# The softmax shift of an attention layer as a 33rd contraction row, with queries and keys stored and loaded as such rows

## The chip, the cores and the metric

The kernel runs on one core of a Trainium2 chip. Its time is the device time of one execution in microseconds, the median of several runs. All arithmetic of four layers is in this one launch; the inputs and the output lie in device memory (HBM).

The core's engines work side by side, each through its own queue in order: PE (TensorE: matrix products, with PEld for its weight loads), DVE (VectorE), ACT (ScalarE), POOL (GpSimd) and SP (SyncE, which here issues nearly all DMAs).

## The reference, cut to what matters

An image of 32 x 32 positions (L = 1024) with C = 256 channels, four images (NB = 4), passes four layers: a convolution with a state-space scan, a grouped convolution, an attention over the 1024 positions with a mixture of experts behind it, and a second scan with a second mixture of experts. The change touches the attention of layer 2 only:

```python
Q, K, V = (proj(Wq, bq), proj(Wk, bk), proj(Wv, bv))      # 8 heads of 32
scores = jnp.einsum('bhnd,bhmd->bhnm', Q, K) / jnp.sqrt(jnp.float32(hd))
mask = jnp.zeros((N, N), dtype=bool).at[edge_index[0], edge_index[1]].set(True)
scores = jnp.where(mask[None, None], scores, -jnp.inf)
attn = jax.nn.softmax(scores, axis=-1)
attended = jnp.einsum('bhnm,bhmd->bhnd', attn, V)
```

The softmax subtracts a number from each query's scores before the exponential. Any number gives the same result as long as nothing overflows. The kernel uses zero, unless a bound on the scores says that they could be large; then it takes the row's maximum.

## The kernel before

**The scans.** Both scans are cut into units of 128 rows x 1024 positions, 1280 in all. A unit takes DVE a product with PE's replicated rows (`ps_rep`) and a running scan (`h<-dA,ps_rep`), ACT an exponential (`dA`), POOL a product, PE two products for `ps_rep` and, every second unit, eight records of collecting products (`ps_y`). Its `dA` is a DMA of 512 KB, loaded four units ahead into one of five buffers. The order of the scans is fixed (`SCANS`, line 32; a pair is layer and image): (0,0), (0,1), (3,0), (0,2), (3,1), (0,3), (3,2), (3,3). A scan of layer 0 has 256 units, one of layer 3 has 64. So (3,3) begins at unit 1216.

**The side stages.** All else is written as Python generators and laid between the units (`STAGES`, line 34): `front` of an image before its first scan; `middle` between its two scans (the end of layer 0, layer 1, attention, experts, and the beginning of layer 3, `front3`); `last` after its second scan (the end of layer 3 and its experts). One stage runs at a time and isn't broken off; when it ends, `advance` (line 598) picks the first stage in the list whose scan is done, or, failing that, one whose scan is far enough. `middle` of image 3 must deliver the inputs of scan (3,3). When they aren't there at unit 1216, `need` (line 583) lays the whole rest of that stage down without scans between; in that stretch, `alone` is set and attention uses the scans' PSUM (`ps_sx` instead of `ps_sc`).

**The clocks kept by hand.** How densely side work is laid between units is decided when the program is written, not on the chip. `Metered` (line 99) adds an estimated cost to a clock per engine for each instruction. `run` (line 620) goes through the scans' half units and calls `advance` at most twice in each, only while no engine's clock is ahead of the vector clock. A tensor product's estimate is `matmul_us`:

```python
us = 0.46e-3 * columns(out)
if lhsT.dtype != BF16:
    us = max(4 * us, 0.3)
if out.shape[0] <= 32:
    return us / 4
return us / 2 if lhsT.shape[0] <= 32 else us
```

**Attention** (`attention`, line 1264). Queries and keys are projected into `qT` and `kT` (128 partitions x 2 x 1024: four heads of 32 rows in each half), the bound on the scores is worked out (`large_scores`), the mask is loaded as additive bf16 tiles (`maskT`), values are projected. POOL then adds two biases. `shift` (line 1406) holds a branch: with small scores nothing is done and `mT`, the shift, stays at zero; with large ones `row_max` fills it, each number split into three bf16 parts in rows of their own. In the traced execution no instruction of `row_max` ran.

`all_heads` (line 1328) then runs 64 steps: two halves of the queries (`nh`), four pairs of heads (`hp`), eight blocks of 128 keys (`kb`). A step of `heads` (line 1478) has on PE: two products of 32 rows for the scores of the pair, two products of 32 rows of ones (`onesb`) with the shift, two of 128 rows that add the mask; ACT takes the exponential into `p`; two steps later four products of `p` with values and with ones, 32 columns each, are summed over the blocks (`ps_at`). SP has nothing to do in these steps but the scans' DMAs.

Of the kernel before, what the change touches and what calls it, by code (L numbers as in the profile page):

```python
# [8 lines left out]
F32 = mybir.dt.float32  # L9
BF16 = mybir.dt.bfloat16  # L10
I32 = mybir.dt.int32
AF = mybir.ActivationFunctionType
ALU = mybir.AluOpType
# [4 lines left out]
P = 128  # L18
NB = 4
L = 1024  # L20
TB = L // P
C = 256
DI = 512
DC = DI // P
HEADS, HD = 8, 32
# [117 lines left out]
class Hybrid:  # L143
# [1092 lines left out]
    def prepare2(self, st):  # L1236

        nc, vec = self.nc, self.vec
        self.gamma, self.beta, self.bo = (self.rows("L2_attn_" + n) for n in ("gamma", "beta", "bo"))
        wo = self.weight(st, "L2_attn_Wo", 2)  # L1240
        yield
        ps = self.ps("ps_bo", (P, C))
        for k in range(2):
            nc.tensor.matmul(
                ps, lhsT=vec["L2_attn_bv"][:, k : k + 1].to_broadcast([P, P]), rhs=wo[:, k, :],
                start=(k == 0), stop=(k == 1),
            )
        nc.vector.tensor_tensor(self.bo, self.bo, ps, ALU.add)
        self.isq = 1.0 / float(HD) ** 0.5
        self.bq = self.const.tile([P, 2], F32, name="bq_")  # L1250
        nc.vector.tensor_scalar(self.bq, vec["L2_attn_bq"], self.isq, None, ALU.mult)

        byhead = st.tile([P, 4], F32, name="byhead4")
        nc.vector.tensor_reduce(
            byhead, self.ident.rearrange("p (h d) -> p h d", d=HD), AX.X, ALU.add
        )
        self.byhead = self.const.tile([P, 4, 8], F32, name="byhead")
        nc.vector.tensor_copy(self.byhead, byhead.unsqueeze(2).to_broadcast([P, 4, 8]))
        self.onesb = self.const.tile([P, P], BF16, name="onesb")
        nc.vector.memset(self.onesb, 1.0)  # L1260
        self.ones = self.const.tile([P, 32], F32, name="ones32")
        nc.vector.memset(self.ones, 1.0)

    def attention(self, b, tb):
        nc, tc, vec = self.nc, self.tc, self.vec
        with tc.tile_pool(name=f"at{b}", bufs=1, side="right") as op:
            xa = op.tile([P, TB, C], F32, name="xa")
            qT = op.tile([P, 2, L], F32, name="qT")
            kT = op.tile([P, 2, L], F32, name="kT")
            v = op.tile([P, TB, C], F32, name="v")  # L1270
            mT = op.tile([P, 2, L], BF16, name="mT")
            maskT = op.tile([P, TB, L], BF16, name="maskT")
            wo = self.weight(op, "L2_attn_Wo", 2)
            large = op.tile([1, 1], I32, name="large")
            nc.vector.memset(mT, 0.0)
            with tc.tile_pool(name=f"aa{b}", bufs=1, side="right") as fp:
                wq, wk, wv = (self.weight(fp, "L2_attn_" + n, 2) for n in ("Wq", "Wk", "Wv"))
                xT = fp.tile([P, 2, L], F32, name="xTa")
                yield from self.norm(fp, tb, TB, xa, "lnt")
                yield from self.turned(xa, TB, xT)  # L1280

                def project(item):
                    w, dst, bias, sc, c, g = item
                    ps = self.ps("ps_qk")
                    cols = slice(g * 512, (g + 1) * 512)
                    self.mm(ps, lambda k: w[:, k, c * P : (c + 1) * P], xT, 2, cols)
                    nc.scalar.activation(
                        dst[:, c, cols], ps, AF.Identity, bias=bias[:, c : c + 1], scale=sc
                    )

                yield from self.pipe(
                    [
                        (w, dst, bias, sc, c, g)
                        for w, dst, bias, sc in (
                            (wq, qT, self.bq, self.isq), (wk, kT, vec["L2_attn_bk"], 1.0)
                        )
                        for c in range(2) for g in range(2)
                    ],
                    project, cost=1.7,
                )  # L1300

                yield from self.large_scores(fp, qT, kT, large)
                for _ in self.mask_work:
                    pass
                nc.sync.dma_start(maskT, self.mem[("maskT",)].rearrange("j p f -> p j f"))

                def values(j):
                    ps = self.ps("ps_v", (P, 2, C))
                    for i in range(2):
                        m = 2 * j + i  # L1310
                        for k in range(2):
                            nc.tensor.matmul(
                                ps[:, i, :], lhsT=xT[:, k, m * P : (m + 1) * P], rhs=wv[:, k, :],
                                start=(k == 0), stop=(k == 1),
                            )
                    nc.scalar.copy(v[:, 2 * j : 2 * j + 2, :], ps)

                yield from self.pipe(range(TB // 2), values, cost=1.7)
            go = nc.values_load(large, engines=self.sides, min_val=0, max_val=1)
            tc.mark_branch_hint_location(f"large{b}", go, engines=self.sides)  # L1320
            yield from self.add_rows(xa, self.bo, TB)
            yield from self.add_rows(tb, self.beta, TB)
            with tc.tile_pool(name=f"ab{b}", bufs=1, side="right") as fp:
                yield from self.shift(fp, qT, kT, mT, maskT, go, f"large{b}")
            with tc.tile_pool(name=f"ac{b}", bufs=1, side="right") as fp:
                yield from self.all_heads(b, fp, tb, qT, kT, v, maskT, mT, xa, wo)

    def all_heads(self, b, fp, tb, qT, kT, v, maskT, mT, xa, wo):
        nc = self.nc

        def divided(raw, sums, c):
# [8 lines left out]
        halves = [  # L1340
            [fp.tile([P, 2, 512], F32, tag=t, name=t, bufs=2) for t in ("raw", "sums")]
            for _ in range(2)
        ]
        scores, values = self.heads(fp, halves, qT, kT, v, maskT, mT)
        for n in range(len(steps) + 2):
            if n >= 2:
                values(steps[n - 2])
# [10 lines left out]
            nh, hp, kb = steps[n - 2]  # L1358
# [58 lines left out]
    def row_max(self, fp, qT, kT, mT, mask):  # L1417


        nc = self.nc  # L1420

        m3 = fp.tile([P, TB, HEADS, 32], BF16, name="m3")
        nc.vector.memset(m3, 0.0)
        mx = fp.tile([P, TB, HEADS, 2], F32, name="mx")
        got = {}
        yield 1.0
# [19 lines left out]
        def largest(item):  # L1446
# [8 lines left out]
            scores, largest, cost=1.4,  # L1455
        )
        m = fp.tile([P, TB, HEADS], F32, name="mneg")
        nc.vector.tensor_reduce(m, mx, AX.X, ALU.max, negate=True)
        for s in range(3):
            nc.vector.tensor_copy(m3[:, :, :, s], m)  # L1460
            if s < 2:
                nc.vector.tensor_tensor(m, m, m3[:, :, :, s], ALU.subtract)
        yield 1.0

        def turn(item):
            c, g = item
            ps = self.ps("ps_m3", dtype=BF16)
            for k in range(4):
                nc.tensor.transpose(
                    ps[:, k * P : (k + 1) * P],  # L1470
                    m3[:, 4 * g + k, 4 * c : 4 * c + 4, :].rearrange("p h s -> p (h s)"),
                    self.identb,
                )
            nc.scalar.copy(mT[:, c, g * 512 : (g + 1) * 512], ps)

        yield from self.pipe([(c, g) for c in range(2) for g in range(2)], turn, cost=0.8)

    def heads(self, fp, halves, qT, kT, v, maskT, mT):

        nc = self.nc
        got, acc = {}, {}

        def scores(step):
            nh, hp, kb = step
            qs = slice(nh * 512, (nh + 1) * 512)
            c, at = hp // 2, 64 * (hp % 2)
            alone = self.alone  # L1490
            if alone:
                both = self.scan_psum.tile([P, 2, 512], F32, tag="x", name="ps_sx", bufs=2)
                two = [both[:, i, :] for i in range(2)]
            else:
                two = [self.psum.tile([P, 512], F32, tag="s", name="ps_sc", bufs=2) for _ in range(2)]
            rows = [slice(at + 32 * i, at + 32 * i + 32) for i in range(2)]
            for i in range(2):
                nc.tensor.matmul(
                    two[i], lhsT=kT[rows[i], c, kb * P : (kb + 1) * P], rhs=qT[rows[i], c, qs],
                    start=True, stop=False,  # L1500
                )
            for i in range(2):
                nc.tensor.matmul(
                    two[i], lhsT=self.onesb[rows[i], :], rhs=mT[rows[i], c, qs],
                    start=False, stop=False,
                )
            got[step] = p = fp.tile([P, 2, 512], F32, tag="p", name="p", bufs=3)
            for i in range(2):
# [659 lines left out]
```

## Time and profile before

| | us |
|---|---|
| median of 3 runs | 6310.74 |
| lowest, highest | 6305.61, 6317.68 |
| profiled execution | 6294.21 |
| span of its instructions | 6292.5 |
| PE, DVE, ACT, POOL busy | 5142.7, 5032.7, 3410.6, 3825.9 |
| 512 records of the shift's products, busy (404 `ps_sc`, 108 `ps_sx`) | 86.1 + 20.6 |
| first and last scores of image 0, 1, 2 | 1400.6 to 1644.2, 2461.9 to 2702.9, 3826.4 to 4071.2 |
| first and last scores of image 3 | 5192.6 to 5388.2 |
| last unit before (3,3), first and last of (3,3) | 5227.8, 5680.7 and 5954.8 |

An f32 product stands in the trace as two records. Busy time of an engine counts overlapping records once. Units can be counted in the trace as scans on DVE (`h<-dA,ps_rep`), and a stage's place in units by the scans that began before its first instruction. Every side instruction carries the line of the helper that meters it (L131), so groups are told apart by the names of their tiles.

### The profile page before, as it was taken

Reading aid. Unit: us, or ns where it says so; the run is one execution under the profiler, and the core shown is the slowest. Engines: PE = TensorE matmul, PEld = TensorE weight load, DVE = VectorE, ACT = ScalarE, POOL = GpSimd, SP = SyncE. Lnnn points to the kernel's source line nnn. Section 1 sums busy time; section 2 is a strip of 40 time slices with the busy share of each in tenths; the row PEclk is TensorE's granted clock in tenths of the full one; section 3 lists DMA queues with packets and bytes.
Section 4 is the critical chain, followed back from the end, with each engine's and each line's share of the span. In section 5 each row is a group of like instructions: output and inputs, shape, how many; then the busy total and the mean of one; then the engine's idle time right before and its main releaser. Section 6 shows DMA issues by size and latency. Waiting matters only on the chain. (4 is left out here: it accounts for less than half of the span.)

```text
span 6292.5 us, 59823 instructions
## 1 busy us (share of the span) xinstructions
PE 5142.7 (82%) x20249; PEld 2117.1 (34%) x20249; DVE 5032.7 (80%) x4016; ACT 3410.6 (54%) x4299; POOL 3825.9 (61%) x1948
## 2 busy tenths in 40 slices
PE   5676785579798568979869969989689779997999
PEld 2122120132253122234225522244145332543566
DVE  5888898988898998889889988899889982317811
ACT  3565655345496435558638735567547544336621
POOL 2787768665586766568767756577867752006600
PEclk7687785589798668979969979979779889999989
DMA  3555555544355656445455576345545761027611
GB/s 109 160 158 167 165 175 185 159 150 136 113 173 177 194 165 170 132 128 191 159 178 174 182 179 165 119 150 195 174 156 179 208 161 48 19 73 184 166 34 34
DMA packets 347915, 934.97 MB, mean 149 GB/s; under 512 B 37748, under 2 KB 120256, under 8 KB 345984
## 3 DMA queue, kind: packets, MB, share of 16 engines
q1 hardware_dynamic: 344880, 928.38, 48.7%
q0 software_dynamic: 2128, 2.13, 0.2%
q8 instruction: 165, 2.70, 0.2%
q14 instruction: 166, 1.36, 0.1%
q10 hardware_dynamic: 576, 0.39, 0.0%
HBM read 841.02 MB, written 92.37 MB: 148 GB/s over the span
## 5 line engine op out<-in xcount | busy, mean ns | idle before, releaser
L131 POOL TENSOR_TENSOR h<-h,rows 128x1024 f32<-128x1024 f32 x1280 | 3024.2, 2366 | 1740.4 <-DVE h L131 1529.3
L131 DVE TENSOR_TENSOR_SCAN h<-dA,ps_rep 128x1024 f32<-128x1024 f32 x1280 | 2924.3, 2285 | 182.2 <-ACT dA L131 53.6
L131 DVE TENSOR_TENSOR ps_rep<-ps_rep,rows 128x1024 f32<-128x1024 f32 x1280 | 1549.4, 1210 | 142.6 <-PE ps_rep L131 141.7
L131 PE MATMUL ps_rep<-S,spread_L_conv_A_log 96*128 96x512 bf16 x2048 | 752.8, 456 | 770.3 <-DVE h L131 722.4
L131 ACT ACTIVATE dA<-dA,A_L_conv_A_log 128x1024 f32<-128x1024 f32 x1024 | 1125.4, 1142 | 440.0 <-DMA dA<-dt 405.7
L131 PE MATMUL ps_y<-h,collect_L_conv_A_log 128*32 128x512 f32 x4096 | 704.4, 741 | 15.3 <-POOL h L131 15.3
L131 PE MATMUL ps_e<-we,h_m 128*128 128x256 f32 x3072 | 709.4, 383 | 8.3 <-ACT h_m L131 8.3
L131 PEld LDWEIGHTS <-spread_L_conv_A_log 96*128 96x128 bf16 x2048 | 159.7, 102 | 1558.0 <-DVE h L131 1246.4
L131 PEld LDWEIGHTS ps_e<-we,h_m 128*128 128x128 f32 x3072 | 583.3, 191 | 159.2 <-ACT h_m L131 31.0
L131 PE MATMUL ps_h<-xTm,we 128*128 128x512 f32 x1280 | 603.3, 607 | 4.6 <-DMA we<-in_L_ffn_W_dram 4.5
L131 ACT ACT_TABLE_LOAD x402 | 515.8, 1283 | 37.0 <-PE ps_h L131 15.5
L131 ACT ACTIVATE h_m<-ps_h,cols 128x512 f32<-128x512 f32 x384 | 257.5, 686 | 423.0 <-PE ps_h L131 421.0
L131 ACT ACTIVATE p<-ps_sc 128x512 f32<-128x512 f32 x404 | 219.3, 594 | 316.7 <-PE ps_sc L131 306.1
L131 ACT ACTIVATE dA<-dA,A_L_attn_A_log 128x1024 f32<-128x1024 f32 x256 | 282.8, 1143 | 141.4 <-DMA dA<-dt 122.8
L131 PEld LDWEIGHTS ps_h<-xTm,we 128*128 128x128 f32 x1280 | 242.2, 193 | 281.0 <-issue 211.5
L131 PE MATMUL ps_rep<-S,spread_L_attn_A_log 96*128 96x512 bf16 x512 | 176.8, 433 | 160.2 <-DVE h L131 138.6
L131 PE MATMUL ps_at<-p,v 128*32 128x512 f32 x1024 | 270.7, 608 | 0.2 <-ACT p L131 0.2
L131 PE MATMUL ps_at<-p,ones 128*32 128x512 f32 x1024 | 270.7, 608 | 0.0
L131 DVE SCALAR_TENSOR_TENSOR tb_rows<-ps_e,cw,tb_rows 128x256 f32<-128x256 f32 x128 | 55.7, 477 | 242.8 <-PE ps_e L131 242.7
L131 PE MATMUL ps_sc<-qT,kT 32*128 32x512 f32 x808 | 244.0, 654 | 4.6 <-ACT p L131 2.0
L131 PE MATMUL ps_cv<-pad,diag 128*128 128x512 f32 x504 | 230.5, 597 | 0.0
L131 PEld LDWEIGHTS ps_y<-h,collect_L_conv_A_log 128*32 128x32 f32 x4096 | 93.2, 118 | 339.7 <-issue 216.6
(347 smaller groups left out, 5475.6 us busy)
## 6 DMA issues: line engine op xcount, KB each, us to landing
dA<-dt SPq DMA_DIRECT2D x1280, 512.0 KB
we<-in_L_ffn_W_dram SPq DMA_DIRECT2D x64, 512.0 KB
parts<-parts SPq DMA_DIRECT2D x60, 384.0 KB
S<-parts SPq DMA_DIRECT2D x90, 256.0 KB
dt<-sp_r SPq DMA_DIRECT2D x64, 256.0 KB
y<-yo SPq DMA_DIRECT2D x128, 128.0 KB
y_back<-y SPq DMA_DIRECT2D x64, 256.0 KB
we<-in_L_ffn_w_dram SPq DMA_DIRECT2D x64, 256.0 KB
```

What stands on the lines that cost most here:

```text
L131: return got(*args, **kw)
```

## The change

Queries and keys go to device memory after they are projected, head by head, in blocks of 33 rows: 32 of the head and one more. For keys that row is one (written once, when the kernel starts); for queries it is the shift, written after `shift`. The scores' product then contracts over 33 rows, and its last row adds the shift. The product of ones with the shift is gone, and so are `onesb`, the bf16 parts of the shift in `row_max`, and the long life of `qT` and `kT`, which now stand in a pool of their own that closes before the heads begin. In `heads`, the rows of two heads are loaded into one tile each for keys and queries, at partitions 0 and 64, when a pair's first block begins: for the next pair, and at the very first step for two pairs.

```diff
-        self.onesb = self.const.tile([P, P], BF16, name="onesb")
-        nc.vector.memset(self.onesb, 1.0)
+        one = st.tile([HEADS, L], F32, name="one_row")
+        nc.vector.memset(one, 1.0)
+        self.k_rows = [self.keep(("k", b), [HEADS, HD + 1, L]) for b in range(NB)]
+        for to in self.k_rows:
+            nc.sync.dma_start(to[:, HD, :], one)
...
+                mT = qp.tile([HEADS, L], F32, name="mT")
+                nc.vector.memset(mT, 0.0)
...
+                    for x, to in ((qT, self.q_rows(b)), (kT, self.k_rows[b])):
+                        for h in range(HEADS):
+                            at = HD * (h % 4)
+                            nc.sync.dma_start(to[h, :HD, :], x[at : at + HD, h // 4, :])
+                    yield from self.large_scores(fp, qT, kT, large)
...
+                with tc.tile_pool(name=f"ab{b}", bufs=1, side="right") as fp:
+                    yield from self.shift(fp, qT, kT, mT, maskT, go, f"large{b}")
+                nc.sync.dma_start(self.q_rows(b)[:, HD, :], mT)
...
+        def load(nh, hp):
+            k = fp.tile([P, L], F32, tag="k_rows", name="k_rows", bufs=2)
+            q = fp.tile([P, 512], F32, tag="q_rows", name="q_rows", bufs=2)
+            for i in range(2):
+                at = slice(64 * i, 64 * i + HD + 1)
+                nc.sync.dma_start(k[at, :], self.k_rows[b][2 * hp + i])
+                nc.sync.dma_start(q[at, :], self.q_rows(b)[2 * hp + i, :, nh * 512 : (nh + 1) * 512])
+            rows[nh, hp] = k, q
...
-            rows = [slice(at + 32 * i, at + 32 * i + 32) for i in range(2)]
+            if kb == 0:
+                at = 4 * nh + hp
+                for g in range(0 if at == 0 else at + 1, min(at + 2, 8)):
+                    load(g // 4, g % 4)
+            k, q = rows[nh, hp]
             for i in range(2):
+                of = slice(64 * i, 64 * i + HD + 1)
                 nc.tensor.matmul(
-                    two[i], lhsT=kT[rows[i], c, kb * P : (kb + 1) * P], rhs=qT[rows[i], c, qs],
-                    start=True, stop=False,
-                )
-            for i in range(2):
-                nc.tensor.matmul(
-                    two[i], lhsT=self.onesb[rows[i], :], rhs=mT[rows[i], c, qs],
-                    start=False, stop=False,
+                    two[i], lhsT=k[of, kb * P : (kb + 1) * P], rhs=q[of, :], start=True, stop=False
                 )
```

More of the change, by code (lines that the diff above doesn't have):

```diff
@@ L1267, in attention @@
             xa = op.tile([P, TB, C], F32, name="xa")
-            qT = op.tile([P, 2, L], F32, name="qT")
-            kT = op.tile([P, 2, L], F32, name="kT")
             v = op.tile([P, TB, C], F32, name="v")
-            mT = op.tile([P, 2, L], BF16, name="mT")
             maskT = op.tile([P, TB, L], BF16, name="maskT")
@@ L1274, in attention @@
             large = op.tile([1, 1], I32, name="large")
[L1275 to L1288, printed above, removed]
-                    )
[L1291 to L1295, printed above, removed]
-                        )
[L1297 to L1308, printed above, removed]
-                    for i in range(2):
-                        m = 2 * j + i
-                        for k in range(2):
-                            nc.tensor.matmul(
[L1313 to L1324, printed above, removed]
+            with tc.tile_pool(name=f"aq{b}", bufs=1, side="right") as qp:
+                qT = qp.tile([P, 2, L], F32, name="qT")
+                kT = qp.tile([P, 2, L], F32, name="kT")
+                mT = qp.tile([HEADS, L], F32, name="mT")
+                nc.vector.memset(mT, 0.0)
+                with tc.tile_pool(name=f"aa{b}", bufs=1, side="right") as fp:
+                    wq, wk, wv = (self.weight(fp, "L2_attn_" + n, 2) for n in ("Wq", "Wk", "Wv"))
+                    xT = fp.tile([P, 2, L], F32, name="xTa")
+                    yield from self.norm(fp, tb, TB, xa, "lnt")
+                    yield from self.turned(xa, TB, xT)
+                    def project(item):
+                        w, dst, bias, sc, c, g = item
+                        ps = self.ps("ps_qk")
+                        cols = slice(g * 512, (g + 1) * 512)
+                        self.mm(ps, lambda k: w[:, k, c * P : (c + 1) * P], xT, 2, cols)
+                        nc.scalar.activation(
+                            dst[:, c, cols], ps, AF.Identity, bias=bias[:, c : c + 1], scale=sc
+                        )
+                    yield from self.pipe(
+                        [
+                            (w, dst, bias, sc, c, g)
+                            for w, dst, bias, sc in (
+                                (wq, qT, self.bq, self.isq), (wk, kT, vec["L2_attn_bk"], 1.0)
+                            )
+                            for c in range(2) for g in range(2)
+                        ],
+                        project, cost=1.7,
+                    )
+                    for x, to in ((qT, self.q_rows(b)), (kT, self.k_rows[b])):
[3 more added lines that the diff above has]
+                    yield from self.large_scores(fp, qT, kT, large)
+                    for _ in self.mask_work:
+                        pass
+                    nc.sync.dma_start(maskT, self.mem[("maskT",)].rearrange("j p f -> p j f"))
+                    def values(j):
+                        ps = self.ps("ps_v", (P, 2, C))
+                        for i in range(2):
+                            m = 2 * j + i
+                            for k in range(2):
+                                nc.tensor.matmul(
+                                    ps[:, i, :], lhsT=xT[:, k, m * P : (m + 1) * P], rhs=wv[:, k, :],
+                                    start=(k == 0), stop=(k == 1),
+                                )
+                        nc.scalar.copy(v[:, 2 * j : 2 * j + 2, :], ps)
+                    yield from self.pipe(range(TB // 2), values, cost=1.7)
+                go = nc.values_load(large, engines=self.sides, min_val=0, max_val=1)
+                tc.mark_branch_hint_location(f"large{b}", go, engines=self.sides)
+                yield from self.add_rows(xa, self.bo, TB)
+                yield from self.add_rows(tb, self.beta, TB)
+                with tc.tile_pool(name=f"ab{b}", bufs=1, side="right") as fp:
+                    yield from self.shift(fp, qT, kT, mT, maskT, go, f"large{b}")
+                nc.sync.dma_start(self.q_rows(b)[:, HD, :], mT)
@@ L1325, in attention, with all_heads @@
             with tc.tile_pool(name=f"ac{b}", bufs=1, side="right") as fp:
-                yield from self.all_heads(b, fp, tb, qT, kT, v, maskT, mT, xa, wo)
-    def all_heads(self, b, fp, tb, qT, kT, v, maskT, mT, xa, wo):
+                yield from self.all_heads(b, fp, tb, v, maskT, xa, wo)
+    def all_heads(self, b, fp, tb, v, maskT, xa, wo):
         nc = self.nc
@@ L1343, in all_heads @@
         ]
-        scores, values = self.heads(fp, halves, qT, kT, v, maskT, mT)
+        scores, values = self.heads(b, fp, halves, v, maskT)
         for n in range(len(steps) + 2):
@@ L1420, in row_max @@
         nc = self.nc
-        m3 = fp.tile([P, TB, HEADS, 32], BF16, name="m3")
-        nc.vector.memset(m3, 0.0)
         mx = fp.tile([P, TB, HEADS, 2], F32, name="mx")
@@ L1458, in row_max, with turn, q_rows, heads @@
         nc.vector.tensor_reduce(m, mx, AX.X, ALU.max, negate=True)
[L1459 to L1462, printed above, removed]
         yield 1.0
-        def turn(item):
-            c, g = item
-            ps = self.ps("ps_m3", dtype=BF16)
+        def turn(g):
+            ps = self.ps("ps_m")
             for k in range(4):
[L1469 to L1478, printed above, removed]
-        nc = self.nc
-        got, acc = {}, {}
+                nc.tensor.transpose(ps[:HEADS, k * P : (k + 1) * P], m[:, 4 * g + k, :], self.ident)
+            nc.scalar.copy(mT[:, g * 512 : (g + 1) * 512], ps[:HEADS, :])
+        yield from self.pipe(range(2), turn, cost=0.8)
+    def q_rows(self, b):
+        if ("q", b) not in self.mem:
+            self.keep(("q", b), [HEADS, HD + 1, L])
+        return self.mem["q", b]
+    def heads(self, b, fp, halves, v, maskT):
+        nc = self.nc
+        got, acc, rows = {}, {}, {}
+        def load(nh, hp):
+            k = fp.tile([P, L], F32, tag="k_rows", name="k_rows", bufs=2)
+            q = fp.tile([P, 512], F32, tag="q_rows", name="q_rows", bufs=2)
+            for i in range(2):
+                at = slice(64 * i, 64 * i + HD + 1)
+                nc.sync.dma_start(k[at, :], self.k_rows[b][2 * hp + i])
+                nc.sync.dma_start(q[at, :], self.q_rows(b)[2 * hp + i, :, nh * 512 : (nh + 1) * 512])
+            rows[nh, hp] = k, q
         def scores(step):
@@ L1488, in scores @@
             qs = slice(nh * 512, (nh + 1) * 512)
-            c, at = hp // 2, 64 * (hp % 2)
             alone = self.alone
@@ L1495, in scores @@
                 two = [self.psum.tile([P, 512], F32, tag="s", name="ps_sc", bufs=2) for _ in range(2)]
-            rows = [slice(at + 32 * i, at + 32 * i + 32) for i in range(2)]
+            if kb == 0:
[3 more added lines that the diff above has]
+            k, q = rows[nh, hp]
             for i in range(2):
+                of = slice(64 * i, 64 * i + HD + 1)
                 nc.tensor.matmul(
-                    two[i], lhsT=kT[rows[i], c, kb * P : (kb + 1) * P], rhs=qT[rows[i], c, qs],
-                    start=True, stop=False,
-                )
-            for i in range(2):
-                nc.tensor.matmul(
-                    two[i], lhsT=self.onesb[rows[i], :], rhs=mT[rows[i], c, qs],
-                    start=False, stop=False,
+                    two[i], lhsT=k[of, kb * P : (kb + 1) * P], rhs=q[of, :], start=True, stop=False
                 )
```

## The prediction

> **What bounds the kernel now.** I read the 40 slices first, then the tile views (when each stage ran), the windows, the waits inside attention, and a timeline of the stretch without scans. From the page:
>
> ```profile
> PE   5676785579798568979869969989689779997999
> DVE  5888898988898998889889988899889982317811
> ```
>
> DVE is nearly full for 33 slices: the scans, 1216 of 1280 units of some 3.54 us. In slices 34 to 36 it is almost idle and PE is full: the last image must pass its middle stage before the last scan (3,3) can start. Then come that scan and a tail of PE. So two things are paid: the time until unit 1216 is done (5230 us), and the bare stretch after it. Windows of attention of image 0, the stage of experts behind it, the wait after that, the middle of image 3 under the scan, and bare attention (columns: window, length, then busy us and instructions of PE, PEld, DVE, ACT, POOL, clock, DMA):
>
> ```profile
> 1400.60:1652.00 251.40, 245.33 (x1400) 65.85 (x1400) 219.37 (x138) 146.96 (x214) 151.66 (x69) 0.99 0.42 131
> 1739.50:1890.00 150.50, 147.26 (x621) 78.89 (x620) 144.17 (x86) 140.93 (x174) 131.61 (x70) 1.00 0.52 170
> 2084.00:2280.00 196.00, 106.23 (x322) 12.54 (x314) 189.60 (x113) 67.94 (x65) 142.10 (x65) 0.52 0.61 191
> 5068.00:5231.50 163.50, 133.48 (x505) 47.09 (x505) 135.73 (x106) 73.35 (x97) 99.07 (x49) 0.79 0.56 142
> 5231.50:5390.00 158.50, 158.32 (x910) 40.00 (x912) 14.43 (x19) 67.21 (x76) 24.80 (x20) 1.00 0.13 32
> ```
>
> The reader is to see: under a scan, attention leaves PE 6 us of 251 and DVE 32, so there PE sets the pace; in bare attention PE is everything; after image 0's middle stage (third row) side work is out and only scans run. Waits of DVE in the first window:
>
> ```profile
> DVE ps_rep L131 <- PE ps_rep L131: 11.2, 14, 3.1
> DVE lny_w L131 <- ACT lny_r L131: 7.0, 1, 7.0
> DVE h L131 <- ACT dA L131: 5.5, 13, 0.7
> DVE sums L131 <- ACT sums L131: 2.6, 1, 2.6
> ```
>
> Only the first, and part of the third, can go with a shorter PE.
>
> **Removed: the product of ones and shift.** One bare step of attention:
>
> ```profile
> 5307.49 1.13 PE L131 MATMUL ps_sx<-qT,kT 32*128 32x512 f32 x4
> 5308.45 0.38 PE L131 MATMUL ps_sx<-mT,onesb 32*128 32x512 bf16 x2
> 5308.76 0.60 PE L131 MATMUL ps_sx<-maskT,identb 128*128 128x512 bf16 x2
> 5309.30 0.62 PE L131 MATMUL ps_at<-p,v 128*32 128x512 f32 x2
> ```
>
> From start to start: scores 0.96, shift 0.31, mask 0.54, and 0.99 to the next step: 2.80 us. The Trainium skill ("TensorE: Matmul & The Clock Gate", Back-to-back issue gap) gives 216 ns to a product of 512 columns on a warm array; that would make the removal worth 64 x 0.22 = 14 us in a bare stage. The row says 0.31, because the pair changes type and weights, so 64 x 0.31 = 20 us. I take the row: a step becomes 2.49.
>
> **Kept, but in 33 rows.** Today the two heads' f32 products run side by side (0.96 for both; one 128-row f32 product, from ps_h, 8 records in 3.43 us, takes 0.86). No row has 33 rows. Ends: 0.96, or one after the other, 2 x 0.86 = 1.72. The skill's "TensorEngine Tiling (Array Packing)", section Row Tiling, speaks against the change here: up to 32 rows the array holds four products, up to 64 only two. But only two are sent, at partitions 0 and 64, so the rule still puts them side by side. I take 0.96; the other end is a rival.
>
> **Moved without being meant: the hand-kept clock.** `matmul_us` (line 86) halves the price when the weights have at most 32 rows. Price now: scores 2 x 0.47, shift 2 x 0.12, mask 2 x 0.24, values 4 x 0.24 = 2.59 per step. With 33 rows each score costs 0.94 and the shift nothing: 3.30. A scan unit gives 3.55 on the vector clock and takes 0.94 of the tensor clock, so 2.61 is left per unit; reciprocals add 13.7 to the vector clock, output products 3.8 to the tensor one. Now: (64 x 2.59 + 3.8 - 13.7) / 2.61 = 60 units; the trace counts 59 scans in the first window. After: (64 x 3.30 - 9.9) / 2.61 = 77. Every attention is spread over 17.3 more units although the real PE work shrinks.
>
> Where that goes, from the first and last starts of ps_qk, ps_dt, ps_o and ps_e: image 0's middle stage ends at unit 457, its scan (3,0) begins at 512 and the next stage at 516: 17 units fit in. Image 1's middle stage runs from 516 to 713, the last stage of image 0 follows to 835, image 2's middle stage starts there (ps_yt at 844), ends at 1041, the last stage of image 1 runs to 1163, image 3's middle stage starts then. No gap in that row, so two stretches of 17.3 add: image 3 starts 34.6 units later. At unit 1216 it stands where it now stands 34.6 units earlier, at about 5068 us, ahead of the second layer's convolution, instead of 8 steps into attention.
>
> **The scans' time to unit 1216.**
> - PE no longer binds attention: 64 x 2.49 + 77 x 1.0 (ps_rep 0.52, half of ps_y's 0.97) + 10 = 246 us of PE against 77 x 3.54 + 28 = 300 of DVE. Of the 11.2 + 5.5 us above I take 14 back per stage: 3 x 14 = 42 us. Bounds 0 and 26 per stage (the four waits in full).
> - The 17.3 added units in images 1 and 2 run at 3.54 (third row: 54 scans in 196 us, with some other work): +122. The 34.6 lost from image 3 cost 163.5 / 36 each, since DVE's and PE's side work stood among them: -157. Image 0's are taken from its idle wait: 0.
> - Sum: -42 - 35 = -77.
>
> **The bare stretch.** What is now done at 5068 to 5195 comes bare. PE rows at full clock: down and convolution 44 records x 0.43, up 16 x 0.215, transposes 4, queries and keys 32 x 0.43, norms 3.5, values 32 x 0.215: 50. Chains in which PE waits: two Relu 3, add and Relu 3, norm 9, transposed copies 1, squares and maxima 5: 21. Cold clock after such waits (0.79 in the fourth row) 5, branch 1, round trip of rows 8: 85 us. Bounds: 59 (PE and one norm), and 109 (the 127 us under the scan, times 120/151, what the experts of images 3 and 0 took bare and covered, + 8). Then 64 steps x 2.49 = 160 in place of 158.5 for the rest of today's steps. Sum: +86.
>
> **Added: the DMAs.** Per image 16 stores of 32 rows, one of the shift, 32 loads of 33 rows, all on SP, which issues one in 0.32 to 0.6 us (its rows): some 20 us, spread. SP waits 174 to 192 us of each attention window for a free dA buffer, so its time is there; but dA is fetched only four units ahead, and the 16 stores wait for ACT's last key and then hold the next dA for some 7 us. Loads of a pair are issued eight steps before use. The first one isn't: store of the shift, then load, with the queue blocked between and PE's in-order queue (ps_rep behind the scores) waiting. The nearest rows are larger: 384 KB stored in 5.22 us and 256 KB loaded in 4.20 on the chain. For 32 KB and 400 KB I take 8 us with the issues; DVE holds one unit ahead, so about 2 us of it show, with 3 from the stores: 5 x 3 = 15 us (bounds 0 and 45). Bare, all 8 show and are in the 85. That 33 rows use 11 of 16 engines (33 divides by 11; "DMA: Bandwidth & Descriptors", Why a DMA increments its semaphore by 16) makes a load of 270 KB some 0.5 us longer, under those eight steps.
>
> **The sum.** -77 + 86 + 15 = +24. The profiled run took 6294.2 us (span 6292.5): it would be 6318. The runs shown have a median of 6310.7, 16 above; the same step puts the median at **6335 us**.
>
> **Rivals.**
> - *33-row products one after the other*: +0.76 a step. Bare 64 x 0.76 = 49; under scans PE needs 295 against DVE's 300, some 6 us a stage, 19. Total +92: 6403. For it: no such row exists. Against: two tiles for two heads. 0.15.
> - *The rows come late each time*: if SP is held by the pair before, each of 32 loads costs 3 us on PE: about +100 more, 6435. Against: the buffer's last reader was issued a step earlier. 0.10.
> - *Faster: the delay doesn't reach image 3.* If the stages between absorb it, what remains is -42 + 15 and bare -56 x 0.31 = -17: -44, 6267. Each unit of delay costs (24 + 44) / 34.6 = 2 us, so it decides from 22 units: if only one stage's 17 arrive, -10, 6301. For it: the bare prologue at its lower bound works the same way. Against: each of those stages starts where the one before ends. 0.25.
> - The forecast, 0.50.
>
> A measurement here tells no change from 0.2%, 12.6 us. Slower: the first two rivals and 0.42 of the forecast, 0.67. Same: 0.07 of the forecast and 0.08 of the faster case, 0.15. Faster: 0.17 of the faster case and 0.01 of the forecast, 0.18. Range: bounds of the forecast (-26, 0, 59, 45) and the nearer part of both sides: 6280 to 6410.
>
> **What would show it.** Right: no ps_sc from onesb; k_rows,q_rows pairs still 0.96 apart from the mask; 76 scans between first and last ps_sc of images 0 to 2, DVE waiting under 5 us on ps_rep there; ps_yt of image 3 near unit 1207; all 64 steps of image 3 as ps_sx, 2.5 us apart, and a bare stretch about 85 us longer, reached some 60 us sooner. Wrong: ps_sx in the first window of image 3 still late at 1216, pairs 1.7 apart, or PE waiting for k_rows at every pair.

## The result and the profile after

The changed kernel takes 6401.33 us (median; 6396.42 to 6406.17), beside 6308.17 for the kernel before in the same runs: ratio **1.0153**, 95% interval 1.0132 to 1.0173, so 93 us slower. The forecast was 6335, 24 slower: right in sign, and about a quarter of the size. The measured time lies inside its range of 6280 to 6410, close to the upper end.

Two lines of the 40 slices of the page after (PE and DVE, busy tenths):

```profile
PE   6676785578788677879869977879869969997999
DVE  5888899989889898989899988989899960217811
```

The bare stretch, where DVE falls to 0 to 2, begins at about the same time as before (5231.1 us, before 5227.8) and is longer by 96 us, six tenths of a slice. Next, three windows of the kernel after: attention of image 0, the bare stretch up to the first scores of image 3, and image 3's attention (window, length, then busy us and instructions of PE, PEld, DVE, ACT, POOL, the granted clock, DMA share, GB/s):

```profile
1416.60:1718.10 301.50, 271.12 (x1368) 62.53 (x1368) 268.89 (x168) 160.28 (x227) 184.41 (x82) 0.92 0.46 147
5231.10:5313.90 82.80, 61.56 (x177) 29.40 (x169) 14.15 (x36) 26.89 (x42) 33.85 (x27) 0.86 0.55 153
5313.90:5490.00 176.10, 175.86 (x912) 40.92 (x912) 14.43 (x19) 76.85 (x85) 8.86 (x7) 0.96 0.05 17
```

From its first scores to its last product with values, image 0's attention takes 301 us instead of 246, and PE now has 30 us free in it. All of image 3's attention lies bare, behind 83 us of its prologue. From the last unit before (3,3) to the first of (3,3) it takes 549.0 us (before 452.9: +96, forecast +86). But that stretch begins at 5231.1 us, where the forecast had it 62 us sooner than before's 5227.8. **These 65 us are most of the miss**: the scans came no sooner.

Three groups of waits in the kernel after bear on it. DVE in image 1's attention (waited for, total us, times, longest), before and after:

```profile
DVE ps_rep L131 <- PE ps_rep L131: 8.5, 14, 2.3
DVE lny_w L131 <- ACT lny_r L131: 7.0, 1, 7.0
DVE h L131 <- ACT dA L131: 5.5, 13, 0.7
```

```profile
DVE ps_rep L131 <- PE ps_rep L131: 20.3, 8, 11.4
DVE lny_w L131 <- ACT lny_r L131: 2.9, 1, 2.9
DVE h L131 <- ACT dA L131: 0.7, 2, 0.4
```

Many small waits have become few and long ones, and the total is no smaller (23.9 us, before 21.0). PE over the whole span, and DVE at the experts' norm over the whole span:

```profile
PE ps_sc L131 <- DMA k_rows<-k: 11.7, 2, 6.4
PE ps_sc L131 <- DMA q_rows<-q: 8.7, 1, 8.7
PE ps_sx L131 <- DMA q_rows<-q: 6.9, 1, 6.9
...
DVE lnm_st L131 <- POOL tb L131: 19.0, 4, 6.5
```

PE waits for rows once per image. The last line was 2.9 us in two waits before, and no step of the prediction speaks of it. How much of the 65 us each group answers for is what the experiments have to tell.

### The profile page after: what moved, and what is told of

Same layout as the page of the kernel before. It is cut to its first block, busy times and chain, and to the rows that moved or that the text cites. A ratio compares the mean times of both kernels' runs of the same rounds, so it can differ in the third digit from the quotient of the medians.

```text
span 6394.7 us, 59170 instructions
## 1 busy us (share of the span) xinstructions
PE 5157.2 (81%) x19737; PEld 2089.2 (33%) x19737; DVE 5039.2 (79%) x4016; ACT 3409.1 (53%) x4295; POOL 3825.9 (60%) x1948
## 5 line engine op out<-in xcount | busy, mean ns | idle before, releaser
L131 PE MATMUL ps_at<-p,v 128*32 128x512 f32 x1024 | 290.9, 649 | 0.2 <-ACT p L131 0.2
L131 PE MATMUL ps_at<-p,ones 128*32 128x512 f32 x1024 | 290.9, 649 | 0.0
L131 PE MATMUL ps_sc<-q_rows,k_rows 33*128 33x512 f32 x768 | 246.8, 689 | 25.8 <-DMA k_rows<-k 11.7
```

What stands on the lines that cost most here:

```text
L131: return got(*args, **kw)
```

## The experiments

Times in one group share their runs of the kernel before: 6303.75 us in the first four, 6301.18 in the next four, 6306.37 in the last four.

### First four: the parts one by one

Theory 1: the dearer price of a 33-row product (plan of the scans, not chip work) makes most of the loss. Theory 2: the rows' way through memory makes it. Where medians of different groups are compared, the ratios to the kernel before are the safer measure; they are given where the two differ.

**The price alone**, on the kernel before: its plan charges what the change's plan charges, its work is untouched.

```diff
             got[step] = p = fp.tile([P, 2, 512], F32, tag="p", name="p", bufs=3)
+            self.clock["tensor"] += 0.46e-3 * 512 * 3
```

> The kernel before, with nothing changed but the plan: every attention step adds 0.71 us to the hand-kept tensor clock, as the 33-row price does. Theory 1 (the dearer price spreads each attention over 17 units, starts image 3's middle stage 35 units later and lays it bare): most of the loss of the change comes back without any of its instructions; first ps_yt of image 3 near unit 1207, bare stretch before scan (3,3) about 95 us longer, total about 6380 to 6400, within 30 us of the changed kernel. Theory 2 (the rows' DMAs and their waits cost the time): the plan alone costs under 30 us, total 6300 to 6340.

6361.45 us, ratio 1.0098 (1.0082 to 1.0115): +58 by the medians. ps_yt of image 3 begins at unit 1208 (before 1172), the bare stretch is 96 us longer, and unit 1216 is reached 32 us sooner. So the price is a large part, though below the range expected; the later start and the longer bare stretch are there without any row.

**The rows alone**: the change with the plan of before.

```diff
-    return us / 2 if lhsT.shape[0] <= 32 else us
+    return us / 2 if lhsT.shape[0] <= 33 else us
...
+            self.clock["tensor"] += 0.46e-3 * 512
```

> The changed kernel with the price of 33 rows halved again and 0.24 us added per step, so that the plan is that of the kernel before. Theory 1: about 6330, from -12 us (56 bare steps x 0.21), +7 (the first load of image 3), and per image under the scan some +9 (round trip of the shift's row minus a shorter step); ps_yt of image 3 at unit 1172. Theory 2: still about 6380 to 6400.

6317.31 us, ratio 1.0024 (1.0011 to 1.0036), nearer to the 6330 of theory 1. Against the changed kernel this is 84 us less (81 by the ratios), for the price alone.

**Half price, nothing in the place of the removed product** (the first of these two edits only):

> The changed kernel with the price of 33 rows halved and nothing else, so that a step is planned at 2.36 us (2.59 before, 3.30 in the changed kernel): 54 units an attention. Theory 1: image 3's middle stage starts 10 units earlier than before (near 1162), the bare stretch is some 35 us shorter than before, but PE binds attention under the scans again (64 x 2.59 + 54 + 10 = 230 us of PE against 219 of DVE), so that scans reach unit 1216 later: total about 6330 to 6350. Theory 2: about 6380 to 6400, as the changed kernel.

6349.05 us, ratio 1.008 (1.0064 to 1.0097). A cheaper price than before's also loses, 32 us against the run just above: attention takes 52 units with PE busy for 226 of image 1's 235 us, and the bare stretch shrinks to 400.5 us (there 445.9) while the last unit before it moves to 5332 (there 5264).

**The removal alone**: the kernel before without the product of ones, its price kept in the plan.

```diff
-            for i in range(2):
-                nc.tensor.matmul(
-                    two[i], lhsT=self.onesb[rows[i], :], rhs=mT[rows[i], c, qs],
-                    start=False, stop=False,
-                )
+            self.clock["tensor"] += 0.46e-3 * 512
```

> The kernel before without the product of ones and shift (the shift by the row maximum is left out of the computation), with 0.24 us per step kept on the tensor clock so that the plan stays. It shows what the removal alone is worth, with 32-row scores and no rows in memory. By the prediction's row (0.31 us a step) a bare step takes 2.49 us, the 56 bare steps give 17 us; by the changed kernel's trace, in which score pair to mask takes 1.06 and not 0.96, it takes 2.59 and they give 12. With PE's hold on the three attentions under scans loosened, 5 to 14 us each: total 6255 to 6282, faster than before under both theories.

6263.2 us, ratio 0.9942 (0.9925 to 0.9958). No shift is applied in it. The removal is worth 40 us (37 by the ratio), and the rows cost 6317.3 - 6263.2 = 54 in its company, not the 15 + 8 of the prediction. That was the open question for the next four.

### Next four: what do the rows cost?

Theory A: PE waits at each image's first pair and starts cold. Theory B: it is the 33rd row and the stores. A timeline of the kernel after at image 1's first pair (start us, us, engine, operation, in brackets the idle time before and its releaser):

```profile
2484.05 0.30 SPq L1495 DMA_DIRECT2D k_rows<-k  x1
...
2486.74 0.35 SPq L1496 DMA_DIRECT2D q_rows<-q  x1
2486.88 3.83 PE L131 MATMUL ps_sc<-q_rows,k_rows 33*128 33x512 f32 x4 [5.32 <-DMA k_rows<-k]
2491.99 2.56 PE L131 MATMUL ps_sc<-q_rows,k_rows 33*128 33x512 f32 x4 [0.31 <-ACT p L131]
2498.07 1.13 PE L131 MATMUL ps_sc<-q_rows,k_rows 33*128 33x512 f32 x4
2498.18 1.23 DVE L131 TENSOR_TENSOR ps_rep<-ps_rep,rows 128x1024 f32<-128x1024 f32 x1 [11.45 <-PE ps_rep L131]
```

SP issues eight loads 0.39 us apart; PE stands still for 5.3 us, then runs its next two pairs in 3.83 us (its second head's rows came later still) and 2.56 us, where the third takes 1.13. The scan's ps_rep comes on PE only after all of it, and DVE loses 11.45 us. In the run of the price alone, which has no rows, DVE loses 5.65 us at this place:

```profile
2476.43 1.23 DVE L131 TENSOR_TENSOR ps_rep<-ps_rep,rows 128x1024 f32<-128x1024 f32 x1 [5.65 <-PE ps_rep L131]
```

So DVE loses 5.8 us more here with the rows. The prediction had the wait (8 us) but let only about 2 us of it show on DVE. The slow pairs are not the rows' doing: with the price alone PE stops for only 1.13 us here and its first two pairs take 2.15 and 2.55 us, and in the kernel before those of image 2 take 2.16 and 2.56 after a stop of 0.30.

**No store in front of the loads** (base: the rows alone): zeros once at the start, a store of the shift only where it isn't zero.

```diff
+            nc.sync.dma_start(self.q_rows(b)[:, HD, :], none)
...
-                nc.sync.dma_start(self.q_rows(b)[:, HD, :], mT)
```

> Base is the changed kernel with the plan of before (6317 us, 54 above the kernel that has neither product nor rows). Here the shift's row of the queries is set to zero once at the start and stored again only inside the branch for large scores, so the loads of the first pair no longer stand behind a store. Theory A (most of the 54 us is PE waiting at the first pair, and its cold clock afterwards): the wait gets shorter by the store's 3.6 us and the cold steps fewer; about 4 us per image, 6300. Theory B (the 54 us lie in the 33rd row and in the stores that hold SP): within 6 us of 6317.

6302.56 us, ratio 1.0002 (0.9993 to 1.0011): 15 us off, as by A.

**And the first pair loaded early:**

```diff
+                load(op, 0, 0, 1)
                 go = nc.values_load(large, engines=self.sides, min_val=0, max_val=1)
...
-                at = 4 * nh + hp
-                for g in range(0 if at == 0 else at + 1, min(at + 2, 8)):
-                    load(g // 4, g % 4)
+                at = 4 * nh + hp + 1
+                if at < 8:
+                    load(fp, at // 4, at % 4)
```

> As e5, and the rows of the first pair are loaded right after the values' projection, ahead of the biases and the branch, into a tile of their own; the second pair's at the first step. Theory A: PE has no wait of 6 to 9 us for q_rows or k_rows any more, DVE none of 10 to 12 us for ps_rep; 4 x 8 us less than the base, about 6285. Theory B: no faster than e5, near 6310.

6287.95 us, ratio 0.9967 (0.9953 to 0.9981): another 15 (22 by the ratios), now faster than before. A, and of about its size: the two steps take 29 us off, and no product of PE waits for rows any more.

**32 of the 33 rows**, every DMA kept:

```diff
-                of = slice(64 * i, 64 * i + HD + 1)
+                of = slice(64 * i, 64 * i + HD)
```

> Base as for e5, every DMA kept, but the scores' products use 32 of the 33 rows, at partitions 0 and 64; the shift is left out of the computation. What the 33rd row costs on PE by itself. If it is the 0.10 us seen in a bare step (1.06 against 0.96): a bare step 2.49 us, 5.6 us less in the bare stretch and at most as much per image under the scans: 6295 to 6312. If the 0.10 comes from the places 0 and 64 and not from the row: bare step 2.59 and 6317.

6320.67 us, ratio 1.0023 (1.0012 to 1.0033), the same as with 33. Bare steps of this kernel, and of the removal alone, where the rows lie at their old places:

```profile
5401.09 1.13 PE L131 MATMUL ps_sx<-q_rows,k_rows 32*128 32x512 f32 x4
5402.15 0.60 PE L131 MATMUL ps_sx<-maskT,identb 128*128 128x512 bf16 x2
```

```profile
5304.43 1.13 PE L131 MATMUL ps_sx<-qT,kT 32*128 32x512 f32 x4
5305.49 0.60 PE L131 MATMUL ps_sx<-maskT,identb 128*128 128x512 bf16 x2
```

1.06 us from pair to mask in both. So the 0.10 that the score pair gained (1.06 us to the next product, 0.96 before) belongs neither to the 33rd row nor to the places 0 and 64, the two causes that the expectation named. What the two kernels share is the step from the f32 pair straight to the mask's bf16 product of 128 rows; before, the product of ones stood between them.

**Rows without loads ahead of the heads**: ACT writes each head to its partitions out of PSUM; only the second half of the queries still goes through memory.

```diff
-                        nc.scalar.activation(
-                            dst[:, c, cols], ps, AF.Identity, bias=bias[:, c : c + 1], scale=sc
-                        )
+                    for r in range(4):
+                        of, to = slice(32 * r, 32 * r + 32), slice(64 * (r % 2), 64 * (r % 2) + 32)
+                        at = dst[to, 2 * c + r // 2, cols] if dst is kT else (qT, q2)[g][to, 2 * c + r // 2, :]
+                        nc.scalar.activation(
+                            at, ps[of, :], AF.Identity,
+                            bias=bias[of, c : c + 1], scale=sc,
+                        )
```

> The 33 rows without loads before the heads: ACT writes each head's 32 rows from PSUM straight to partitions 0 or 64 (four copies of 32 rows in place of one of 128), row 33 comes from a constant in memory ahead of the projections, the second half of the queries waits in memory (2 stores, 8 loads with some 24 steps to spare). Squares are taken from PSUM, tile y takes the place of the sums, prices as before. Theory A: nothing of the wait is left; the kernel without product and rows (6263) plus 64 x 0.10 us bare and part of that under scans, plus some us for ACT's 30 us more per image: 6270 to 6285, so faster than before. Theory B (33rd row most of the 54): 6300 or more.

6325.79 us, ratio 1.0033 (1.0023 to 1.0043): a miss for theory A, and no case for B, since the run with 32 of the 33 rows is no faster. From first projection to first scores of image 1 it takes 74.3 us against 58.7 in the removal alone, for two scan units more, and the other images show the same. ACT is busy 47.2 us there instead of 29.6, and DVE waits for what stands behind ACT: 9.2 us for ps_n (3.0 in the removal alone) and 7.9 for dA (none). This version also moved the norms between the projections, so which of the two did it stays open.

In this kernel, and in the removal alone, the stretch from the last ps_at to the first expert takes 93 to 95 us as before; in all the others with rows so far it takes 99 to 104. That is the wait for POOL's tb: in the kernel after

```profile
2821.35 1.26 POOL L131 TENSOR_TENSOR tb<-tb,y_at 128x512 f32<-128x512 f32 x1
2822.64 0.43 DVE L131 BATCH_NORM_STATS2 lnm_st<-tb 128x6 f32<-128x256 f32 x1 [4.17 <-POOL tb L131]
```

The first statistics need only the first rows of tb, ready for long; they wait for the last. In the program with the first pair early that instruction waits on POOL's and ACT's counters; in that of the removal alone it doesn't. The reason lies in the addresses of the two programs. The pool of the experts' norm opens on memory just freed. Before, it lies over attention's own pool alone. Without qT, kT and the old mT that pool is 20 KB per partition shorter (its low end at byte 186304 of each partition in the kernel with the rows alone, at 165824 in the removal alone, the norm's pool at 178528 in both), so the norm's pool reaches over the pool of the heads, and y_at in it (bytes 181984 to 186080) is read last by POOL.

### Last four: memory, and price again

**The pools apart** (base: no store in front of the loads):

```diff
+            op.tile([P, 1952], F32, name="apart")
             xa = op.tile([P, TB, C], F32, name="xa")
```

> As e5_row_at_start (6302.6), and an unused tile of 7.8 KB at the low end of attention's pool, so that the pool of the experts' norm, which opens when attention closes, lies over that pool alone again, as it does before, and not over the pool of the heads, where y_at is read last by POOL. Theory: the first statistics of that norm (lnm_st) wait for POOL's last tb only because of this place in memory (22 us of DVE in four waits, against 3 before); so these waits go, the stretch from the last ps_at to the experts is 93 to 94 us again, and the time is some 18 to 25 less: about 6281. Rival (the extra 6 to 10 us there come from the phase of the plan or from DMAs): 6302.

6290.67 us, ratio 0.9973 (0.9965 to 0.9982). The stretch takes 93 to 94 us again, and the norm's wait for POOL falls from 22.0 us to 3.0; 12 us less by the medians, 18 by the ratios.

**First pair early and pools apart** (a tile of 416 columns):

> As e6_first_pair_early (6288) with an unused tile of 1.7 KB for the same purpose. If wait at the first pair and place in memory are the whole of what the rows cost with the plan kept (54 us), the time comes to that of the kernel with neither product nor rows (6263) plus 5 us for bare steps of 2.59 us: about 6269. If stores, loads or the 33rd row cost something else too: 6280 or more.

**6264.5 us, ratio 0.9935 (0.9921 to 0.9948)**: faster than both kernels. DVE's waits at the norm in it:

```profile
DVE lnm_st L131 <- POOL tb L131: 2.9, 2, 1.6
```

With the plan of before, then, these two waits are all that the rows cost: the other stores, the loads and the 33rd row together come to nothing that can be measured (6264.5 against 6263.2 without them; ratios 0.9935 and 0.9942, with overlapping intervals). PE at image 1's first pairs in it:

```profile
2461.49 2.36 PE L131 MATMUL ps_sc<-q_rows,k_rows 33*128 33x512 f32 x4 [1.02 <-ACTq L1433]
2465.12 2.56 PE L131 MATMUL ps_sc<-q_rows,k_rows 33*128 33x512 f32 x4 [0.31 <-ACT p L131]
```

The stop is gone and the two pairs are still slow.

**The same with the change's own price:**

> As e9_early_and_apart, with the price as the change has it (a 33-row product not halved): what the dearer price costs when the rows cost nothing. Theory 1: the plan alone costs what it cost without rows, 58 us: about 6327. Rival: 84 us, as between the changed kernel and its twin with the plan of before, so 6353.

6345.91 us, ratio 1.0065 (1.0052 to 1.0079): 81 us for the price, close to the rival's 84. Without the removal it was 58. The two don't add: the plan that thins attention takes away the PE-bound stretch in which the removal would pay.

**The same with the cheap price:**

> As e9_early_and_apart, with 33-row products at half price and nothing charged in the removed product's place: 2.36 per step in place of 2.59, so (64 x 2.36 - 9.9) / 2.61 = 54 scan units for an attention in place of 60. Two such stretches bring image 3 some 11.5 units earlier; at 2 us each 23 less: about 6246. Rival: PE (64 x 2.59 + 54 + 10 = 230 us against 54 x 3.54 + 28 = 219 of DVE) sets the pace and takes that back: 6269 or more.

6299.68 us, ratio 0.9986 (0.9977 to 0.9995), 35 slower than with the plan of before, as by the rival. DVE in image 1's attention of this kernel:

```profile
DVE ps_rep L131 <- PE ps_rep L131: 25.3, 20, 6.0
```

Before's price is the best of the three tried with these rows: in the kernel with the first pair early and the pools apart the same wait is 9.1 us.

## Why the prediction was wrong in size

Three steps lead from the kernel before to the changed one: price +58 (to the price alone), then the removal under that plan -16 (to the rows free of waits with their own price, 6345.9), then the rows' two waits +55 (to the changed kernel). By the ratios they are +62, -21 and +55. That they come to about the 93 measured is no check of its own, since each step starts where the last one ends. Against the forecast's +24 most of the miss lies in two terms: 42 us for a PE that no longer binds, of which 8 came, and 23 us for the rows, which cost 55.

- **Right: the price and where its units go.** 74 units per attention (predicted 77), ps_yt of image 3 at unit 1208 (1207), all 64 steps bare. The prologue took 82.8 us (85). "-35" for units added and lost: the price alone reaches unit 1216 32 us sooner. (The 56 bare steps of the prediction were 54 in the trace before, 10 steps under the scan and not 8; this is under 1 us.)
- **Right: 33-row products side by side.** That rival is out, and so is the one of rows late at every pair: PE waits once an image.
- **Failed: "PE no longer binds attention ... 14 back per stage".** Taking the prediction's 3.54 us off each stretch of attention (first scores to last ps_at, images 0 to 2) for every unit in it leaves what is not scan: in the rows free of waits with their own price this is 1.4, 0.4 and 5.8 us less than before, 8 in place of 42. A PE that is free on the average (35 of image 1's 299 us there) is still late at some places: DVE waits 14.6 us for ps_rep in that stretch, in six waits, where the prediction had under 5. With the plan of before, the removal alone gives 9.7, 7.1 and 9.4 in the same stretches. I had counted a gain of the one plan in the other.
- **Failed: the rows, "5 x 3 = 15" and 8 bare.** 55 in place of 23. One part is the first pair: "about 2 us of it show" was too little; under the price's plan 5.8 us showed in image 1, and with the plan of before the two steps that remove the wait gave 29 us, 7 per image. The 3 us for the stores did not show at all. The other part is a place in memory, which was not in the sum at all (23 us with the plan of before, from the first pair early to first pair early and pools apart; how the 55 divide under the dearer price was not measured): the diff shortens the life of qT and kT, and I priced that at nothing without asking what the next pool would then lie on. That a load of 33 rows runs on 11 engines, as the prediction has it, no trace here shows.
- **Not in the sum: the stages behind attention.** From last ps_at to the first expert the price alone adds 5.8, 6.1 and 6.1 us, with the norm's wait for POOL as before; the change adds 9.9, 11.0 and 10.6. Of the price's 6 in image 1, 4.5 are more work of DVE in the same stretch (busy 82.1 us instead of 77.6), with 17 units in both; no run took them apart further.
- **Wrong by a third: the product of ones at 0.31 us.** A bare step went from 2.80 to 2.59, in the kernel after

```profile
5350.92 1.13 PE L131 MATMUL ps_sx<-q_rows,k_rows 33*128 33x512 f32 x4
5351.98 0.61 PE L131 MATMUL ps_sx<-maskT,identb 128*128 128x512 bf16 x2
...
5353.51 0.70 PE L131 MATMUL ps_sx<-q_rows,k_rows 33*128 33x512 f32 x2
```

5353.51 - 5350.92 = 2.59. The 0.21 is the 216 ns that the Trainium skill gives ("TensorE: Matmul & The Clock Gate", Back-to-back issue gap), which I set aside for the row. The row held two things: the product, and 0.10 us that stay when it goes, 64 x 0.10 = 6 us in the bare steps. The first of these steps took back about as much again: the granted clock is 0.58 over the first 16 us of the bare steps, where it is 1.00 with the price alone, and from the first product of scores to the last the changed kernel takes 174.0 us against 180.8. The 64 shorter steps gave 7 us there and not 13. The rows free of waits have the same slow start (0.55 over 15 us), so it is not the wait for rows that makes it; what does stays open.

## What to carry to other kernels

When work is removed from an engine, ask whether the schedule that follows is still one in which that engine is late; a gain measured under one plan can't be added to the price of another, and a cost model that was tuned with the kernel must be looked at whenever an operand changes shape. A tile whose life ends earlier moves everything that is allocated after it, so look at which tile the next stage's first instruction lies on and who reads that last. Loads that an engine needs first, with other work queued behind, belong ahead of the branch and not behind it: moving four of them per image took 15 us off, and made a kernel that was no faster than before into a faster one.

## What the runs showed that was not expected

PE's first pairs of an attention run slowly whether or not it had to stop for them. In image 1 the second pair took 2.56 us in the kernel after, behind a stop of 5.3 us, and 2.56 us in the kernel with the first pair early and the pools apart, behind one of 1.02; later pairs take 1.13. The granted clock over an attention goes with how much of it PE is idle: in image 1 it is 1.00 before (idle 1% of the time), 0.98 with the first pair early and the pools apart (4%), and 0.91 and 0.93 in the kernel after and in the rows free of waits with their own price (9% and 12%). These windows show that the two go together in the main; that the looser plan lowers the clock is a reading of them, and no run varied one without the other. A contraction over 33 rows, at partitions 0 and 64, took exactly as long as one over 32.
